# Softmax sums of four units collected in one tile, heads turned two units at a time

## The chip, the cores and the metric

The kernel runs on one core of a Trainium2 chip. The metric is the device time of one execution in microseconds (us); lower is better. PE is TensorE, DVE is VectorE, ACT is ScalarE, POOL is GpSimd, SP is SyncE, which issues DMAs.

## The reference

The kernel computes one pre-norm transformer block in fp32: eight sequences of 1024 tokens, width 512, 16 heads of 32 channels. The attention is a differential one. Queries and keys of a head are cut into two halves of 16 channels, and each half gets its own softmax:

```python
h = layernorm(x)
q, k, v = split(h @ w_qkv)
a1 = softmax(q1 @ k1.T * scale)
a2 = softmax(q2 @ k2.T * scale)
out = (a1 - lam * a2) @ v               # per head: 1024 x 32
out = out / rms(out) * norm_w * 0.2     # rms over the 32 channels
x = x + reshape(out) @ wo
x = x + ffn(layernorm(x))               # ternary weights, relu squared, a low-rank branch
```

The change concerns the step from the unnormalised products `exp(scores) @ v` and the sums of the exponentials to `a1 @ v - lam * a2 @ v`.

## The kernel before

**Units.** Attention is cut into 256 units: one head and one half (512) of the queries of one sequence. A sequence ("batch" below) has 32 units. Unit u belongs to batch u // 32; i stands for u % 32. Four units (two heads) are one group n = u // 4; a group ends in one tile `og` that is normalised (`rms_squares`, `rms_sums`, `rms_apply`) and multiplied by `wo` (`output_rows`).

**Blocks.** A unit has eight key chunks kc. The loop takes two chunks at a time, so a unit is four blocks, and a block issues on PE, in this order: scores and their shift for two chunks (`exp_scores`, L267, for both softmaxes), between them four products of the maximum search of two units ahead (`max_scores`, L207), then what the order of the work has put in this slot, then the products with v (`values`, L290) of the block before. ACT takes the exponentials from PSUM (L273). DVE reduces the maximum products (L218, four per block). POOL adds the four `e` tiles of a unit up to `es` (`add_up`, L283 and L285, three additions per unit; two in the light units).

**Slots.** All engines but SP run in the order that the program writes (`manual_schedule`). In the slot behind kc 0 and 1 of a unit there stand, in this order: a step of the next batch's preparation if it is a long one (`project`, L157, or `value_tile`, L145: eight matmul instructions), `max_turn` (L232), `heads_out` (L324), steps of the group's normalisation (`later`), `sums` (L290), and a short step of the preparation (`turn_tile`, L137). The PE part of each is issued there; the part that empties its PSUM bank ("post": copies, L165, L236, L237, L334 to L347) is issued on ACT and DVE behind the whole slot, in the same order. i = 18 to 30 have a projection in this slot; 4, 6, 8, 10, 12, 14, 16 and 17 a value tile; the odd units from 3 to 15 a turn. Units with i = 16, 20, 24, 28 have a second step behind kc 4. The last batch (units 224 to 255) prepares only the first FFN tokens. It has light units, the odd ones and the last three, whose POOL sum leaves out the fourth `e` tile; PE takes that tile itself in `sums`.

**PSUM.** `one_bank()` takes one of four banks (pool `a_ps_1`). Scores, projections, turns, sums and heads share these four; a tile may be written when the last reader of the tile that had its bank is done. The maximum products have three banks of their own, `acc` one.

**The path of the sums.** `sums(u)` multiplies `es` by a tile of ones of 32 columns. With the queries in four quarters along the partitions this gives 128 x 256 sums, each repeated in 32 rows. ACT copies them to SBUF next to the unnormalised heads (`avs`, two halves of 256). `heads_out(u)` turns both halves with four transposes (two for the heads, two for the sums); DVE takes reciprocals (two), multiplies (two) and adds (one) into `og`. `sums(v)` stands in the slot of unit v + 2, `heads_out(v)` in that of v + 3; for a light v they stand behind kc 2 of v + 1 and in v + 2. A group's normalisation begins behind kc 6 of the unit in which its fourth `heads_out` stands.

Of the kernel before, what the change touches and what calls it, by code (L numbers as in the profile page):

```python
# [8 lines left out]
F32 = mybir.dt.float32  # L9
F32R = mybir.dt.float32r  # L10
AF = mybir.ActivationFunctionType
# [6 lines left out]
P = 128  # L18
# [6 lines left out]
def block_phases(  # L25
# [14 lines left out]
    nc = tc.nc  # L40
    B, S, E = x.shape
    H, HD = norm_w.shape
# [3 lines left out]
    HS = S // 2  # L46
    SCALE = float(HD) ** -0.5
    NU = B * H * 2
    ident, neg_half = consts
# [3 lines left out]
    p_s = ctx.enter_context(tc.tile_pool(name="a_s", bufs=4))  # L53
# [10 lines left out]
    wo_sb = p_wo.tile([P, KC, E], F32, name="wo_sb")  # L64
    nw = p_wo.tile([P, NHP], F32, name="nw")
    one_nlam = p_wo.tile([P, 1], F32, name="one_nlam")
    ones = p_wo.tile([P, HD], F32, name="ones")
    wv = wpool.tile([P, KC, E], F32, tag="wv", name="wv")
    nc.gpsimd.memset(ones, 1.0)

    one2 = wpool.tile([P, P], F32R, name="one2")
    nms = [wpool.tile([P, HS], F32R, name=f"nms{i}") for i in range(3)]
# [31 lines left out]
    def one_bank():  # L104
        return ps_1.tile([P, 512], F32, tag="one", name="one")
# [142 lines left out]

    e_of, es_of, acc_of, avs_of = {}, {}, {}, {}

    def exp_scores(u, kc, between=None):

# [20 lines left out]
    def light(u):  # L275

        return u >= NU - 2 * H and (u % 2 == 1 or u >= NU - 3)
# [9 lines left out]
    def quarters(out, w, e, start, stop):  # L287

        for g in range(4):
            nc.tensor.matmul(  # L290
                out[32 * g : 32 * g + 32, :], w,
                e[:, g // 2, (g % 2) * (HS // 2) : (g % 2 + 1) * (HS // 2)],
                start=start, stop=stop,
            )
# [8 lines left out]
        )  # L303

    def evict(u):
        avs_of[u] = p_s.tile([P, 2, HS // 2], F32, tag="avs", name="avs", bufs=4)

        nc.scalar.activation(avs_of[u][:, 0, :], acc_of.pop(u), AF.Copy, scale=one_nlam)

    def sums(u):  # L310
        ps = one_bank()
        es = es_of.pop(u)
        parts = [t[:, i] for t in ((es, e_of[u, 3]) if light(u) else (es,)) for i in range(2)]
        for i, part in enumerate(parts):
            quarters(ps[:, 0 : HS // 2], ones, part, i == 0, i == len(parts) - 1)
        return lambda: nc.scalar.copy(avs_of[u][:, 1, :], ps[:, 0 : HS // 2])

    def heads_out(u):

        avs = avs_of.pop(u)  # L320
        to = one_bank()
        for i in range(2):
            for c in range(2):
                nc.tensor.transpose(  # L324
                    to[:, (2 * i + c) * P : (2 * i + c + 1) * P],
                    avs[:, i, c * P : (c + 1) * P], ident,
                )

        def post():

            parts = to.rearrange("p (i c s a d) -> p i s c a d", i=2, c=2, s=2, a=2)
            rc = p_s.tile([P, 2, 2, 2], F32, tag="rc", name="rc")
            for sm in range(2):
                nc.vector.reciprocal(rc[:, sm], parts[:, 1, sm, :, :, 0])  # L334
            o2 = p_s.tile([P, 2, 2, HD], F32, tag="o2", name="o2", bufs=2)
            for sm, o in enumerate((parts[:, 0, 0], o2)):
                nc.vector.tensor_mul(
                    o, parts[:, 0, sm],
                    rc[:, sm].rearrange("p c (a o) -> p c a o", o=1)
                    .to_broadcast([P, 2, 2, HD]),  # L340
                )
            n = u // 4
            if u % 4 == 0:
                og_of[n] = p_o.tile([P, 4, P], F32, tag="og", name="og")
            col = (u % 4) * HD
            og = og_of[n][:, :, col : col + HD]
            nc.vector.tensor_add(  # L347
                og.rearrange("p (a c) d -> p c a d", a=2), parts[:, 0, 0], o2
            )

        return post

# [234 lines left out]
    adds, outs = {}, {}  # L587
    for v in range(NU):
        adds.setdefault((v + 1, 2) if light(v) else (v + 2, 0), []).append(v)
        outs.setdefault((v + 2, 0) if light(v) else (v + 3, 0), []).append(v)  # L590
    done = None
    ctx.enter_context(tc.manual_schedule(engines=engines))
    with tc.tile_pool(name="a_e", bufs=5) as p_e, tc.tile_pool(name="a_es", bufs=2) as p_es:
        for s in range(0, NS * NU + 2, 2):
            u, kc = divmod(s, NS)
            um, im = divmod(s + AHEAD, NS)
            if done is not None:
                evict(done)
                done = None
            if u > NU - 2 * H and kc == 0:  # L600
                prep.fetch()
            if u == NU - 1 and kc == 0:

                m1 = nms[(NU - 3) % 3].rearrange("p (k r) -> p k r", k=KC)
                nc.sync.dma_start(
                    m1.bitcast(F32), prep.m1_d.rearrange("p k i r -> p k (i r)")
                )
            if um < NU:
                if im == 0 and um + 1 < NU:
                    if um % 2 == 1:  # L610
                        load_keys(um // 2 + 1)
                    load_queries(um + 1)
                between, first = max_scores(um, im, apart=True)
            else:
                between = first = None
            if u < NU:
                if u % (2 * H) == 0 and kc == 0:
                    assert not fill
                    fill = prepare(u // (2 * H) + 1) if u + 2 * H < NU else prepare_tokens()
                exp_scores(u, kc, between=between)  # L620
                if first:
                    first()
                exp_scores(u, kc + 1)
                add_up(u, kc)
            reduce = max_scores(um, im + 1) if um < NU else None
            posts = []

            if fill and (kc == 0 or kc == 4 and u % (2 * H) >= H and u % 4 == 0):
                prepare_step, long = fill.pop(0)
            else:  # L630
                prepare_step = None
            if prepare_step and long:
                posts.append(prepare_step())
            if kc == 0 and um <= NU:
                posts.append(max_turn(um - 1))
            for v in outs.pop((u, kc), []):
                posts.append(heads_out(v))
                if v % 4 == 3:
                    n = v // 4
                    later[u, 6] = lambda n=n: rms_squares(n)  # L640
                    later[u + 1, 0] = lambda n=n: rms_sums(n)
                    later[u + 1, 2] = lambda n=n: rms_apply(n)
                    later[u + 2, 4] = lambda n=n: output_rows(n)
            if (u, kc) in later:
                posts.append(later.pop((u, kc))())
            for v in adds.pop((u, kc), []):
                posts.append(sums(v))
            if prepare_step and not long:
                posts.append(prepare_step())
            if reduce:  # L650
                reduce()
            if 2 <= s < NS * NU + 2:
                uv, kv = divmod(s - 2, NS)
                values(uv, kv)
                values(uv, kv + 1)
                if kv == NS - 2:
                    done = uv
            for post in posts:
                if post:
                    post()  # L660
        evict(done)
        whole(lambda: sums(NU - 1))
    assert not later and list(adds.values()) == list(outs.values()) == [[NU - 1]]

# [104 lines left out]
    def output(g, ys, tiles=range(4)):  # L769
# [16 lines left out]

    n = NU // 4 - 1
    rest = {
        0: lambda: heads_out(NU - 1), 1: lambda: rms_squares(n), 2: lambda: rms_sums(n),
        3: lambda: rms_apply(n),  # L790
        5: lambda: output_rows(n, lambda: ps_mx.tile([P, 512], F32, tag="mx", name="py")),
    }
    low_rank(0)

# [319 lines left out]
```

## Time and profile before

| what | value |
|---|---|
| runs (three) | 5340.47, 5342.63, 5344.19 us; median 5342.63 us |
| span of the profiled execution | 5338.5 us, 4.1 us under that median (its own time outside the span is not recorded) |
| PE busy | 5280.1 us (99%), 41522 matmuls |
| POOL busy | 4121.0 us (77%) |
| DVE busy | 3787.7 us (71%) |
| ACT busy | 2832.5 us (53%) |
| attention loop, first to last exponential | 140.0 to 4261.4 us |
| one batch of 32 units in the middle | 522.3 us |

"Busy" counts the time in which at least one instruction of the engine ran. A matmul's recorded duration contains its way through the array, and matmuls overlap: what a matmul costs is read from the distance between starts. "x16" behind a row of the timeline means that 16 instructions of the same line were merged, and the second column is then the time from the first's start to the last's end.

### The profile page before, as it was taken

Reading aid. Unit: us, or ns where it says so; the run is one execution under the profiler, and the core shown is the slowest. Engines: PE = TensorE matmul, PEld = TensorE weight load, DVE = VectorE, ACT = ScalarE, POOL = GpSimd, SP = SyncE. Lnnn points to the kernel's source line nnn. Section 1 sums busy time; section 2 is a strip of 40 time slices with the busy share of each in tenths; the row PEclk is TensorE's granted clock in tenths of the full one; section 3 lists DMA queues with packets and bytes.
Section 4 is the critical chain, followed back from the end, with each engine's and each line's share of the span. In section 5 each row is a group of like instructions: output and inputs, shape, how many; then the busy total and the mean of one; then the engine's idle time right before and its main releaser. Section 6 shows DMA issues by size and latency. Waiting matters only on the chain.

```text
span 5338.5 us, 105587 instructions
## 1 busy us (share of the span) xinstructions
PE 5280.1 (99%) x41522; PEld 3243.9 (61%) x41522; DVE 3787.7 (71%) x7599; ACT 2832.5 (53%) x5502; POOL 4121.0 (77%) x1495
## 2 busy tenths in 40 slices
PE   8999999999999999999999999999999999999999
PEld 4555555555555555555555555555555578888887
DVE  6877787777778777877777777777888645555554
ACT  4665566566656665666566656655666522222221
POOL 0898899889988998899899989998888733333333
PEclk9999999999999999999999999999999999999999
DMA  8112211211121112111211121112211101111111
GB/s 275 47 55 74 71 50 55 75 66 55 54 77 65 52 57 77 64 55 56 75 65 50 60 81 57 56 61 78 100 48 44 50 31 32 32 32 32 32 32 32
DMA packets 185246, 328.48 MB, mean 62 GB/s; under 512 B 33312, under 2 KB 55840, under 8 KB 184112
## 3 DMA queue, kind: packets, MB, share of 16 engines
q1 hardware_dynamic: 183824, 319.12, 18.3%
q8 instruction: 329, 5.39, 0.4%
q0 software_dynamic: 544, 2.10, 0.1%
q14 instruction: 165, 1.35, 0.1%
q10 hardware_dynamic: 384, 0.52, 0.0%
HBM read 209.16 MB, written 112.46 MB: 60 GB/s over the span
## 4 chain that ended last, share of the span: by engine, by line
PE 84%; POOL 11%; DVE 3%; issue 1%; ACT 1%; DMA 0%; SPq 0%; POOLq 0%; DVEq 0%; ACTq 0%
PE acc L290 15%; PE one L267 14%; PE mx L207 13%; PE y L763 9%; PE pf L744 8%; PE one L157 8%; POOL es L285 6%; PE one L290 4%; PE one L145 4%; PE one L383 3%; POOL es L283 3%; PE one L324 2%; DVE nm L218 1%; PE pf L748 1%; POOL ss L369 1%
## 5 line engine op out<-in xcount | busy, mean ns | idle before, releaser
L218 DVE TENSOR_REDUCE nm<-mx 128x1 f32<-128x512 f32 x4096 | 2550.3, 683 | 256.6 <-PE mx L207 251.5
L273 ACT ACTIVATE e<-one 128x512 f32<-128x512 f32 x4096 | 2116.5, 603 | 803.2 <-PE one L267 751.1
L285 POOL TENSOR_TENSOR es<-es,e 128x2048 f32<-128x2048 f32 x495 | 2261.3, 4568 | 63.2 <-ACT e L273 31.1
L207 PE MATMUL mx<-tk,tq 64*128 64x512 f32 x4096 | 1453.1, 444 | 6.2 <-DVE nm L218 5.6
L283 POOL TENSOR_TENSOR es<-e 128x2048 f32<-128x2048 f32 x256 | 1169.6, 4569 | 278.3 <-ACT e L273 278.2
L267 PE MATMUL one<-nms,one 64*128 64x512 f32 x4096 | 1175.8, 420 | 5.1 <-ACT e L273 2.7
L290 PE MATMUL acc<-e,v 128*32 128x256 f32 x16384 | 1092.7, 384 | 0.0
L207 PEld LDWEIGHTS mx<-tk,tq 64*128 64x128 f32 x4096 | 750.9, 184 | 549.0 <-DVE nm L218 312.3
L267 PE MATMUL one<-tq,tk 64*128 64x512 f32 x4096 | 1063.6, 392 | 0.0
L753 POOL TENSOR_TENSOR r<-r 128x512 f32<-128x512 f32 x256 | 268.4, 1050 | 639.2 <-ACT r L752 618.8
L290 PEld LDWEIGHTS acc<-e,v 128*32 128x32 f32 x16384 | 450.0, 109 | 433.7 <-issue 179.0
L267 PEld LDWEIGHTS one<-tq,tk 64*128 64x128 f32 x4096 | 580.2, 185 | 82.6
L752 ACT ACTIVATE r<-pf,s_fc 128x512 f32<-128x512 f32 x256 | 176.1, 688 | 794.6 <-PE pf L748 544.2
L267 PEld LDWEIGHTS one<-nms,one 64*128 64x128 f32 x4096 | 515.2, 184 | 80.5 <-DVE og L347 15.5
L763 PE MATMUL y<-wpr,r 128*128 128x512 f32 x2048 | 523.3, 397 | 3.7 <-DVE r L757 1.7
L756 DVE CAST r<-r 128x512 fp32r<-128x512 f32 x256 | 180.4, 705 | 425.9 <-POOL r L753 425.9
L157 PE MATMUL one<-hT,wqk 128*128 128x512 f32 x1024 | 475.4, 607 | 1.5 <-ACT hT L138 1.5
L763 PEld LDWEIGHTS y<-wpr,r 128*128 128x128 f32 x2048 | 375.0, 188 | 98.6 <-DVE o L773 20.1
L744 PE MATMUL pf<-hTh,wfc 128*128 128x512 f32 x1024 | 398.8, 389 | 0.0
L744 PE MATMUL pf<-hTl,wfc 128*128 128x512 f32 x1024 | 398.6, 389 | 0.0
L165 DVE SCALAR_TENSOR_TENSOR pc<-one,pc 128x512 fp32r<-128x512 f32 x128 | 88.5, 692 | 350.9 <-ACT pc L164 350.9
L157 PEld LDWEIGHTS one<-hT,wqk 128*128 128x128 f32 x1024 | 185.0, 190 | 217.3 <-issue 187.9
(137 smaller groups left out, 4284.1 us busy)
## 6 DMA issues: line engine op xcount, KB each, us to landing
qk<-pc SPq DMA_DIRECT2D x128, 512.0 KB
tq<-qk SPq DMA_DIRECT2D x512, 128.0 KB
tk<-qk SPq DMA_DIRECT2D x256, 256.0 KB
xs<-in_L_attn_x SPq DMA_DIRECT2D x64, 256.0 KB
xr<-in_L_attn_x SPq DMA_DIRECT2D x256, 64.0 KB
x_dram<-y SPq DMA_DIRECT2D x64, 256.0 KB
out<-o SPq DMA_DIRECT2D x248, 64.0 KB
nms<-md SPq DMA_DIRECT2D x512, 4.0 KB
```

The source lines that it names most:

```text
L145: nc.tensor.matmul(pv, hT_of[b][:, kc, c * P : (c + 1) * P], wv[:, kc, :], start=(kc == 0), stop=(kc == KC - 1),)
L157: nc.tensor.matmul(ps, wqk[:, kc, c0 : c0 + P], hT_of[b][:, kc, tok], start=(kc == 0), stop=(kc == KC - 1),)
L207: nc.tensor.matmul(mx[sm], tq[rows, c * P : (c + 1) * P], tk[rows, kh * 512 : kh * 512 + 512], start=True, stop=True,)
L218: nc.vector.tensor_reduce(nm_of[u][:, kh, sm, c : c + 1], mx[sm], AX.X, ALU.max, negate=True)
L267: nc.tensor.matmul(st[sm], w[rows, cols], m[rows, :], start=(w is one2), stop=(w is not one2))
L273: nc.scalar.activation(e[:, kc % 2, sm, :], st[sm], AF.Exp)
L283: nc.gpsimd.tensor_add(es_of[u], e_of[u, 0], e)
L285: nc.gpsimd.tensor_add(es_of[u], es_of[u], e)
L290: nc.tensor.matmul(out[32 * g : 32 * g + 32, :], w, e[:, g // 2, (g % 2) * (HS // 2) : (g % 2 + 1) * (HS // 2)], start=start, stop=stop,)
L744: nc.tensor.matmul(pf, w[:, kc, :], hT, start=(kc == 0 and i == 0), stop=False)
L753: nc.gpsimd.tensor_mul(r, r, r)
L763: nc.tensor.matmul(ys[i], r2[:, i * P : (i + 1) * P], prep.wpr[j // (NJ // 2)][:, j % (NJ // 2), :], start=(j == 0 and k == 0), stop=(j == ...
```

## The change

The ones become four blocks of 32 columns. In block k only columns 8k to 8k + 7 are one. `sums(u)` uses block u % 4, so that the sums of unit u stand in rows 8k to 8k + 7 of each quarter and zeros in the others. The first unit of a group is copied to a tile `ssum` by ACT; the other three are added to it by DVE from PSUM. `sums_out(n)` turns `ssum` with two transposes and takes all reciprocals of the group in one DVE instruction of 128 x 32. `heads_out` turns two units at a time (four transposes) and multiplies them together: two multiplications of 128 x 256 in place of four of 128 x 128, and two additions into `og`, as before. `sums_out` and the first `heads_out` of group n stand in the slot of unit 4n + 6, the second `heads_out` in that of unit 4n + 7, and the normalisation begins one unit later than before, so that `output_rows` falls in units with u % 4 = 1 and not 0. In light groups all three stand in unit 4n + 5. After the last unit they are spread over the first steps of the FFN.

```diff
-    ones = p_wo.tile([P, HD], F32, name="ones")
+    ones = p_wo.tile([P, 4, HD], F32, name="ones")
-    nc.gpsimd.memset(ones, 1.0)
+    nc.gpsimd.memset(ones, 0.0)
+    for k in range(4):
+        nc.gpsimd.memset(ones[:, k, 8 * k : 8 * k + 8], 1.0)
...
     def evict(u):
-        avs_of[u] = p_s.tile([P, 2, HS // 2], F32, tag="avs", name="avs", bufs=4)
-        nc.scalar.activation(avs_of[u][:, 0, :], acc_of.pop(u), AF.Copy, scale=one_nlam)
+        avs_of[u] = p_s.tile([P, HS // 2], F32, tag="avs", name="avs", bufs=5)
+        nc.scalar.activation(avs_of[u], acc_of.pop(u), AF.Copy, scale=one_nlam)
...
-            quarters(ps[:, 0 : HS // 2], ones, part, i == 0, i == len(parts) - 1)
-        return lambda: nc.scalar.copy(avs_of[u][:, 1, :], ps[:, 0 : HS // 2])
+            quarters(ps, ones[:, u % 4], part, i == 0, i == len(parts) - 1)
+        def post():
+            n = u // 4
+            if u % 4 == 0:
+                ssum_of[n] = p_s.tile([P, HS // 2], F32, tag="ssum", name="ssum", bufs=2)
+                nc.scalar.copy(ssum_of[n], ps)
+            else:
+                nc.vector.tensor_add(ssum_of[n], ps, ssum_of[n])
+        return post
+    def sums_out(n):
+        ss = ssum_of.pop(n)
+        ts = one_bank()
+        for c in range(2):
+            nc.tensor.transpose(ts[:, c * P : (c + 1) * P], ss[:, c * P : (c + 1) * P], ident)
+        def post():
+            rc_of[n] = p_s.tile([P, 4, 2, 4], F32, tag="rc", name="rc", bufs=2)
+            nc.vector.reciprocal(
+                rc_of[n].rearrange("p k c g -> p c g k"),
+                ts[:, 0 : 2 * P].rearrange("p (c g k r) -> p c g k r", c=2, g=4, k=4)[..., 0],
+            )
+        return post
...
     def heads_out(u):
-        avs = avs_of.pop(u)
+        n, k = divmod(u, 4)
         to = one_bank()
         for i in range(2):
+            avs = avs_of.pop(u + i)
             for c in range(2):
                 nc.tensor.transpose(
                     to[:, (2 * i + c) * P : (2 * i + c + 1) * P],
-                    avs[:, i, c * P : (c + 1) * P], ident,
+                    avs[:, c * P : (c + 1) * P], ident,
                 )
...
-        outs.setdefault((v + 2, 0) if light(v) else (v + 3, 0), []).append(v)
+        if v % 4 == 3:
+            n, soon = v // 4, light(v)
+            outs.setdefault((v + 2, 0) if soon else (v + 3, 0), []).extend(
+                [lambda n=n: sums_out(n), lambda v=v: heads_out(v - 3)]
+            )
+            outs.setdefault((v + 2, 0) if soon else (v + 4, 0), []).extend(
+                [lambda v=v: heads_out(v - 1), n]
+            )
...
     rest = {
-        0: lambda: heads_out(NU - 1), 1: lambda: rms_squares(n), 2: lambda: rms_sums(n),
-        3: lambda: rms_apply(n),
-        5: lambda: output_rows(n, lambda: ps_mx.tile([P, 512], F32, tag="mx", name="py")),
+        0: lambda: sums_out(n), 1: lambda: heads_out(NU - 4), 2: lambda: heads_out(NU - 2),
+        3: lambda: rms_squares(n), 4: lambda: rms_sums(n), 5: lambda: rms_apply(n),
+        7: lambda: output_rows(n, lambda: ps_mx.tile([P, 512], F32, tag="mx", name="py")),
     }
```

More of the change, by code (lines that the diff above doesn't have):

```diff
@@ L247, in max_turn @@
         return post
-    e_of, es_of, acc_of, avs_of = {}, {}, {}, {}
+    e_of, es_of, acc_of, avs_of, ssum_of, rc_of = {}, {}, {}, {}, {}, {}
     def exp_scores(u, kc, between=None):
@@ L305, in evict @@
     def evict(u):
-        avs_of[u] = p_s.tile([P, 2, HS // 2], F32, tag="avs", name="avs", bufs=4)
-        nc.scalar.activation(avs_of[u][:, 0, :], acc_of.pop(u), AF.Copy, scale=one_nlam)
+        avs_of[u] = p_s.tile([P, HS // 2], F32, tag="avs", name="avs", bufs=5)
+        nc.scalar.activation(avs_of[u], acc_of.pop(u), AF.Copy, scale=one_nlam)
     def sums(u):
-        ps = one_bank()
+        ps = one_bank()[:, 0 : HS // 2]
         es = es_of.pop(u)
@@ L325, in heads_out @@
                     to[:, (2 * i + c) * P : (2 * i + c + 1) * P],
-                    avs[:, i, c * P : (c + 1) * P], ident,
+                    avs[:, c * P : (c + 1) * P], ident,
                 )
         def post():
[L331 to L336, printed above, removed]
+            parts = to.rearrange("p (m s a d) -> p s m a d", m=4, s=2, a=2)
+            rc = rc_of[n].rearrange("p k c (s a) -> p s (k c) a", s=2)[:, :, 2 * k : 2 * k + 4]
+            o2 = p_s.tile([P, 4, 2, HD], F32, tag="o2", name="o2", bufs=1)
+            for sm, o in enumerate((parts[:, 0], o2)):
                 nc.vector.tensor_mul(
-                    o, parts[:, 0, sm],
-                    rc[:, sm].rearrange("p c (a o) -> p c a o", o=1)
-                    .to_broadcast([P, 2, 2, HD]),
-                )
-            n = u // 4
-            if u % 4 == 0:
+                    o, parts[:, sm],
+                    rc[:, sm].rearrange("p m (a o) -> p m a o", o=1)
+                    .to_broadcast([P, 4, 2, HD]),
+                )
+            if k == 0:
                 og_of[n] = p_o.tile([P, 4, P], F32, tag="og", name="og")
[L345 to L349, printed above, removed]
+            for i in range(2):
+                og = og_of[n][:, :, (k + i) * HD : (k + i + 1) * HD]
+                nc.vector.tensor_add(
+                    og.rearrange("p (a c) d -> p c a d", a=2),
+                    parts[:, 0, 2 * i : 2 * i + 2], o2[:, 2 * i : 2 * i + 2],
+                )
         return post
@@ L589, in block_phases @@
         adds.setdefault((v + 1, 2) if light(v) else (v + 2, 0), []).append(v)
-        outs.setdefault((v + 2, 0) if light(v) else (v + 3, 0), []).append(v)
+        if v % 4 == 3:
[5 more added lines that the diff above has]
+                [lambda v=v: heads_out(v - 1), n]
+            )
     done = None
@@ L635, in block_phases @@
                 posts.append(max_turn(um - 1))
[L636 to L639, printed above, removed]
+            for turn in outs.pop((u, kc), []):
+                if callable(turn):
+                    posts.append(turn())
+                else:
+                    n = turn
                     later[u, 6] = lambda n=n: rms_squares(n)
@@ L662, in block_phases @@
         whole(lambda: sums(NU - 1))
-    assert not later and list(adds.values()) == list(outs.values()) == [[NU - 1]]
+    assert not later and list(adds.values()) == [[NU - 1]] and len(outs) == 1
     HID, R, NJ = prep.HID, prep.R, prep.NJ
```

## The prediction

> **What bounds the kernel now.** I read the page first, then busy time by stretches, then the timeline of single slots. About 0.2% of 5342.63 us, 10.7 us, is what a measurement of this kernel can tell from no change.
>
> ```profile
> PE 5280.1 (99%) x41522; PEld 3243.9 (61%) x41522; DVE 3787.7 (71%) x7599; ACT 2832.5 (53%) x5502; POOL 4121.0 (77%) x1495
> 1157.69:1447.50 289.81, 287.02 (x2621) 162.98 (x2615) 229.50 (x476) 187.19 (x365) 283.85 (x96) 1.00 0.17 52
> 1447.50:1680.22 232.72, 232.72 (x1933) 130.86 (x1935) 169.05 (x342) 132.89 (x260) 194.69 (x49) 1.00 0.22 75
> ```
>
> The second and third line are two stretches of one batch: length, then busy time of PE, PEld, DVE, ACT, POOL. In the first (i = 30 to i = 17 of the next batch) POOL works 283.85 of 289.81 us without a gap over 0.1 us; in the second (i = 18 to 30) it has 38 us to spare and PE none. Where POOL sets the pace, it does so through the `e` tiles: i = 10 of batch 2 starts its exponentials when POOL's last addition of i = 8 ends (1321.21 + 4.59 = 1325.80):
>
> ```profile
> 1321.21 4.59 POOL L285 TENSOR_TENSOR es<-es,e 128x2048 f32<-128x2048 f32 x1
> 1325.90 1.09 ACT L273 ACTIVATE e<-one 128x512 f32<-128x512 f32 x2 [0.66 <-PE one L267]
> ```
>
> Next the slot of unit 50 (i = 18, a projection ahead of it):
>
> ```profile
> 935.34 0.27 PE L232 MATMUL one<-ident,nm 128*8 128x128 f32 x1
> ...
> 935.45 0.60 PE L324 MATMUL one<-ident,avs 128*128 128x128 f32 x4
> 935.54 0.60 ACT L164 ACTIVATE pc<-one 128x512 fp32r<-128x512 f32 x1 [2.54 <-PE one L157]
> ...
> 935.98 1.07 PE L290 MATMUL one<-es,ones 128*32 128x256 f32 x16
> 936.17 0.69 DVE L165 SCALAR_TENSOR_TENSOR pc<-one,pc 128x512 fp32r<-128x512 f32 x1 [3.05 <-ACT pc L164]
> ...
> 937.08 0.28 DVE L237 TENSOR_TENSOR mt<-one,mt 8x128 fp32r<-8x128 f32 x1
> 937.29 0.23 DVE L334 RECIPROCAL rc<-one 128x4 f32<-128x4 f32 x2
> 937.55 0.30 DVE L337 TENSOR_TENSOR one<-one,rc 128x128 f32<-128x128 f32 x1
> ...
> 937.84 0.49 PE L207 MATMUL mx<-tk,tq 64*128 64x512 f32 x1
> ...
> 937.88 0.29 DVE L337 TENSOR_TENSOR o<-one,rc 128x128 f32<-128x128 f32 x1
> 938.21 0.29 DVE L347 TENSOR_TENSOR og<-one,o 128x128 f32<-128x128 f32 x1
> 938.42 0.68 DVE L218 TENSOR_REDUCE nm<-mx 128x1 f32<-128x512 f32 x1
> ```
>
> Call 935.34 T0. Four transposes take 935.98 - 935.45 = 0.53 us of PE, 0.133 each. The next block starts at T0 + 2.50, DVE's first maximum 0.58 us behind it. An undisturbed block takes 2.70 us with that distance 0.54; the maximum products have three banks, so what DVE starts later than 0.54 is added to the block. In the last batch this already costs 1.27 us (1.81 - 0.54; the block is 3.97 long), since two units are turned in one slot:
>
> ```profile
> 3984.01 1.15 PE L324 MATMUL one<-ident,avs 128*128 128x128 f32 x8
> 3986.09 0.49 PE L207 MATMUL mx<-tk,tq 64*128 64x512 f32 x1
> 3987.90 2.47 DVE L218 TENSOR_REDUCE nm<-mx 128x1 f32<-128x512 f32 x4
> 3990.06 0.50 PE L207 MATMUL mx<-tk,tq 64*128 64x512 f32 x1
> ```
>
> **The change, part by part.** Below "0" to "3" is u % 4.
>
> *Transposes.* 1024 become 640; 384 x 0.133 = 51 us of PE go. By slot: units 0 and 1 lose four (-0.53; -0.59 where no long step stands ahead), unit 2 gains the two of `sums_out` (+0.27), unit 3 is as before.
>
> The Trainium skill ("TensorE: Matmul & The Clock Gate", Part 4) gives about 275 ns for a transpose in a kernel. The rows' durations agree (278 ns), but their starts are 133 ns apart; by the page 106 us would go, and I keep 51.
>
> *Copies and DVE.* 192 ACT copies of 0.37 us go, on an engine that waits for PE. DVE gets 192 additions and loses half of its small multiplications. The nearest row to a 256-wide one is
>
> ```profile
> L549 DVE TENSOR_TENSOR hTl<-wb,hTh 128x256 fp32r<-128x256 f32 x120 | 45.0, 417 | 0.0
> ```
>
> against 300 and 292 ns for 128 (L337): +0.13 us for 128 more. So 0.43 and 0.42 for the multiplications, 0.42 for the addition; bounds 0.30 (no cost by width) and 0.60 (twice). The reciprocal of 128 x 32 is near L334's 151 ns: 0.18 (0.15 to 0.3).
>
> *Unit 2 with a projection (i = 18, 22, 26, 30): a fifth bank.* Projection, maximum, sums turned, heads turned and sums want five banks, and there are four. The changed program's first product of `sums` waits for the projection's own second reader, L165: it ends at 936.86, T0 + 1.52, and a waiting PE starts 0.05 later (the median of such waits), T0 + 1.57. Six transposes would let it start at T0 + 0.11 + 0.80 = 0.91. Behind it on PE are the sums, `values` and all later blocks. Cost 0.66, with the transposes 0.93, less 0.04 of DVE lateness that PE's delay covers: +0.89. Bounds: +0.23, if the bank came free in time, to +1.0 with a cold start of the weight loads (0.11). Value tiles have one reader, ACT, ready at T0 + 0.84: no wait.
>
> *Unit 3 with a projection (i = 19, 23, 27): a longer DVE queue.* Behind L237 (T0 + 2.02) stand two multiplications, two additions and the addition of the sums: 0.43 + 0.42 + 0.29 + 0.29 + 0.42 with 0.03 between, to T0 + 4.02. The first maximum overlaps the end by 0.08 and starts at T0 + 3.94, where T0 + 2.50 + 0.54 was due: 0.90 late. Before it was 0.10 late there (the group's `ss` reduction stood in the same slot). +0.80; bounds +0.41 and +1.29 from the widths.
>
> The Trainium skill ("Perfetto Trace Analysis", Optimizing Scalar/DVE Operations) speaks for grouping where the engine is saturated, and for breaking up instructions where it isn't but causes bubbles elsewhere. This DVE is 71% busy and is the second case.
>
> *Units 0 and 1 with a projection.* DVE is free at T0 + 2.4, the block (now T0 + 1.97) needs it at 2.51: -0.53 and -0.04 of old lateness, -0.57 each. Without a projection DVE is free sooner.
>
> *Normalisation one unit later.* `output_rows` (3.6 us of PE) leaves the unit that has two projections; its four loads and its store pass SP's key and query loads of one unit, with DMA engines 22% busy and no one waiting. POOL's `rms_apply` (0.21 + 2.92 + 1.05 = 4.2 us) moves behind the first addition of the next unit; between i = 30 and i = 6, 6 and 10, 10 and 14 POOL has as many of them as before. Zero.
>
> **Sums.** Batches 1 to 6, from POOL's first addition of i = 30 to the start of i = 10: POOL's chain is unchanged, 0. From i = 10 to 14 the units take 62.29 us, POOL's additions for them 62.02; PE alone would fall to 61.4, so POOL decides: -0.27. i = 14 to 17: +0.27, 0, -0.53, -0.53. i = 18 to 29: 3 x (0.89 + 0.80 - 0.57 - 0.57) = +1.65. i = 30: +0.89. Sum +1.48, six times +8.9.
>
> Batch 0 starts without POOL's backlog: three groups of 0.27 - 0.53 - 0.59 = -0.85 instead of -0.27: 1.48 + 0.27 - 2.55 = -0.8.
>
> Last batch: unit 3 loses eight transposes and its wait, -1.08 - 1.34 = -2.42. In unit 1 DVE has the reciprocal and both pairs one behind the other: from T0 + 1.81 0.18 + 2 x 1.43 with 0.03 between, less two overlaps of 0.08, first maximum at T0 + 4.94 instead of 4.15, +0.79. Six groups -9.8. POOL's light sum of unit 231 ends at 3913.49 and PE uses it at 3915.78; with PE 2.42 sooner POOL holds it by 0.2: six times, +1.2. The first units -1.0: 227 turns one pair less (-0.53 and 1.1 of DVE), 228 no longer waits for POOL (-0.43), 229 has +1.04. Unit 255 -2.4, 256 -0.5. In the FFN stand ten transposes for four (+0.8) and an estimated 0.5 for their banks. Sum -11.2.
> Total 8.9 - 0.8 - 11.2 = -3.1. The profiled 5338.5 becomes 5335.4, with the 4.1 around it 5339.5; I say 5339, on its own 5330 to 5350.
>
> **Rivals.**
> (1) *One of the new waits doesn't come*, because the order of readers is kinder than I read it. Without the fifth bank's wait 28 x 0.66 = 18 us less (5321); without DVE's lateness 21 x 0.90 = 19 less (5320); without either 5302. For it: PE is 99% busy, and by that row alone 51 us should go. Against: the program's own wait, and L165's end at T0 + 1.52.
> (2) *The wide DVE instructions cost twice the narrow ones*; slower. The queue of unit 3 grows by 0.17 + 0.16 + 0.16 = 0.49, 21 times; in the last batch 0.66, seven times; i = 15 becomes 0.34 late, seven times: +17, 5357. It decides from 0.57 us per instruction on. Against: the 417 ns above.
> (3) *The last batch gives nothing back*, since POOL's light sums hold PE as soon as it is faster: +11, 5350. Against: they had 2.3 us to spare, so most of the 2.42 should come.
> That the sums are not collected is excluded: the changed program has 640 of these transposes.
>
> **How the numbers follow.** Forecast 0.55, (1) 0.25, (2) 0.13, (3) 0.07. Faster: (1) and the low edge of the forecast, 0.30. Slower: (2) and the upper edges, 0.19. Same: 0.51. The range reaches to one wait missing and to (2): 5318 to 5356; both waits missing lies outside.
>
> **What would show it.** Batches of 523 to 525 us in the middle (522.3 before); the four units from i = 18 longer by about 0.5 than 70.7; in unit 2 with a projection, the sums' first product 0.05 behind the end of the projection's second reader; in i = 19 a first block of 3.6 us; i = 6 to 10 still 62.2; groups of 56.6 us in the last batch (58.1 before). I am wrong if i = 18 to 30 gets shorter (a wait missing), if the first stretch of POOL opens gaps, or if 128 x 256 takes over 0.5 us.

## The result

The changed kernel takes 5350.83 us (median of 19 runs, 5348.65 to 5353.27), the kernel before 5340.69 us beside it (19 runs, 5338.77 to 5346.14). The ratio is 1.0018, with a 95% interval of 1.0011 to 1.0025: slower, by ten microseconds, with 384 transposes taken away (51 us of PE by the prediction's estimate). The profiled execution spans 5349.1 us, 10.6 more than before's 5338.5.

These are the first lines of the page and the chain of waits by engine, after the change:

```profile
PE 5245.8 (98%) x41138; PEld 3211.3 (60%) x41138; DVE 3779.9 (71%) x7087; ACT 2761.0 (52%) x5310; POOL 4123.0 (77%) x1499
PE 75%; POOL 18%; DVE 3%; issue 2%; ACT 1%; DMA 0%; SPq 0%; POOLq 0%; DVEq 0%; ACTq 0%
```

384 instructions are gone from PE and its busy time fell by 34 us, but the span grew: PE now waits. The chain runs over PE for 75% of the span (84% before) and over POOL for 18% (11% before). That is half of the story. The other half is in the lengths of the parts, from the first exponential of one batch to that of the next:

| part (us) | before | after | difference | forecast |
|---|---|---|---|---|
| up to the first exponential | 140.03 | 140.20 | +0.2 | 0 |
| batch 0 | 509.76 | 511.05 | +1.3 | -0.8 |
| batches 1 to 6, mean | 522.24 | 524.48 | +2.24, six times 13.4 | +1.48, six times 8.9 |
| batch 7, to its last exponential | 478.15 | 469.68 | -8.5 | together |
| the rest (feed-forward) | 1077.07 | 1081.25 | +4.2 | -11.2 |

To see what sets a batch's length, cut it where POOL begins the first addition of a unit. Two windows, first of before, then of after: unit 0 to unit 16 of batch 4, and unit 18 to unit 30. The columns are the length, then busy time of PE, PEld, DVE, ACT, POOL, each with its instructions, the granted clock, the DMA share and GB/s.

```profile
2230.96:2478.26 247.30, 244.80 (x2240) 139.17 (x2237) 196.10 (x405) 161.64 (x315) 242.22 (x83) 1.00 0.17 52
2507.69:2719.90 212.21, 212.21 (x1742) 118.75 (x1742) 152.64 (x310) 119.77 (x234) 176.47 (x45) 1.00 0.22 76
```

```profile
2235.14:2482.46 247.32, 241.44 (x2216) 137.79 (x2214) 195.43 (x374) 156.59 (x303) 242.24 (x82) 1.00 0.17 52
2516.28:2730.57 214.29, 212.04 (x1724) 115.95 (x1724) 152.57 (x286) 116.47 (x225) 176.60 (x45) 1.00 0.22 76
```

In the first window the length is the same to 0.02 us, with POOL busy for all but the 5 us between its instructions: PE's work falls by 3.4 us and all of it becomes PE's waiting. In the second, PE's work is hardly less, 2.2 us of waiting are new, and the stretch is 2.1 us longer. So nothing was gained where PE got less to do, and time was lost where PE decides.

**Unit 2 with a projection.** The timeline of the same slot that the prediction showed, unit 50:

```profile
936.30 0.27 PE L234 MATMUL one<-ident,nm 128*8 128x128 f32 x1
...
936.63 0.60 PE L352 MATMUL one<-ident,avs 128*128 128x128 f32 x4
937.13 0.69 DVE L167 SCALAR_TENSOR_TENSOR pc<-one,pc 128x512 fp32r<-128x512 f32 x1 [3.06 <-ACT pc L166]
...
937.97 1.07 PE L292 MATMUL one<-es,ones 128*32 128x256 f32 x16 [0.74 <-DVE pc L167]
...
939.69 0.49 DVE L371 TENSOR_TENSOR og<-one,o 128x128 f32<-128x128 f32 x2
939.83 0.49 PE L209 MATMUL mx<-tk,tq 64*128 64x512 f32 x1
940.36 0.69 DVE L220 TENSOR_REDUCE nm<-mx 128x1 f32<-128x512 f32 x1 [0.19 <-PE mx L209]
```

The fifth bank is there: the first product of `sums` waits 0.74 us for the projection's second reader L167 and starts 0.15 behind its end. The block is 8.78 us long (7.75 before), +1.03.

**Unit 3 with a projection.** DVE's queue in the slot of unit 51, whose next block begins at 955.71 on PE:

```profile
955.15 0.41 DVE L362 TENSOR_TENSOR one<-one,rc 128x256 f32<-128x256 f32 x1
955.60 0.42 DVE L362 TENSOR_TENSOR o<-one,rc 128x256 f32<-128x256 f32 x1
956.06 0.49 DVE L371 TENSOR_TENSOR og<-one,o 128x128 f32<-128x128 f32 x2
956.47 0.41 DVE L325 TENSOR_TENSOR ssum<-one,ssum 128x256 f32<-128x256 f32 x1
956.80 1.88 DVE L220 TENSOR_REDUCE nm<-mx 128x1 f32<-128x512 f32 x3
```

The maximum starts 1.09 behind the block where 0.54 is undisturbed, and the block is 3.25 us long (2.81 before): +0.44. By groups, the mean duration in ns being the number behind the bar and the busy time:

```profile
L325 DVE TENSOR_TENSOR ssum<-one,ssum 128x256 f32<-128x256 f32 x192 | 79.0, 411 | 57.2 <-PE one L292 57.2
L362 DVE TENSOR_TENSOR o<-one,rc 128x256 f32<-128x256 f32 x128 | 54.4, 425 | 4.4
L338 DVE RECIPROCAL rc<-one 128x32 f32<-128x32 f32 x64 | 21.6, 337 | 0.0
```

**The end.** Unit 255's wait for POOL, and the granted clock behind it (last but two column of the windows, ahead of the DMA share):

```profile
4254.38 1.54 PE L292 MATMUL one<-es,ones 128*32 128x256 f32 x16 [3.90 <-POOL es L287]
4255.68 1.95 PE L292 MATMUL one<-e,ones 128*32 128x256 f32 x16
```

```profile
4245.00:4250.00 5.00, 5.00 (x53) 2.58 (x51) 0.00 (x0) 4.52 (x11) 4.75 (x5) 1.00 0.00 0
4254.38:4258.80 4.42, 4.42 (x50) 2.16 (x50) 0.43 (x1) 0.00 (x0) 4.42 (x1) 0.61 0.00 0
```

Sixteen products take up to 1.95 us here; in other places they take 1.07. The kernel before has the same wait, shorter, and behind it slow products and a clock of 0.67 too:

```profile
4248.33 1.94 PE L290 MATMUL one<-es,ones 128*32 128x256 f32 x16 [1.84 <-POOL es L285]
4248.33:4252.50 4.17, 4.17 (x50) 1.97 (x51) 0.00 (x0) 0.37 (x1) 4.17 (x1) 0.67 0.00 0
```

In the feed-forward part PE's first products for `y` waited 1.94 us before, for their own operands. Now they wait for posts of `heads_out` that stand on DVE behind casts, and the granted clock falls behind these waits (last line):

```profile
4282.42 0.69 DVE L790 TENSOR_TENSOR r<-r,r 128x512 fp32r<-128x512 f32 x1
4283.03 0.43 DVE L362 TENSOR_TENSOR one<-one,rc 128x256 f32<-128x256 f32 x1
...
4284.58 0.71 PE L796 MATMUL y<-wpr,r 128*128 128x512 f32 x2 [2.35 <-DVE og L371]
...
4286.97 1.19 PE L796 MATMUL y<-wpr,r 128*128 128x512 f32 x2 [1.68 <-DVE og L371]
4286.97:4292.39 5.42, 5.42 (x13) 4.26 (x14) 0.00 (x0) 0.35 (x1) 0.00 (x0) 0.50 0.01 3
```

### The profile page after: what moved, and what is told of

It is laid out like the page before. It is cut to its first block, busy times and chain, and to the rows that moved or that the text cites. A ratio compares the mean times of both kernels' runs of the same rounds, so it can differ in the third digit from the quotient of the medians.

```text
span 5349.1 us, 104112 instructions
## 1 busy us (share of the span) xinstructions
PE 5245.8 (98%) x41138; PEld 3211.3 (60%) x41138; DVE 3779.9 (71%) x7087; ACT 2761.0 (52%) x5310; POOL 4123.0 (77%) x1499
## 4 chain that ended last, share of the span: by engine, by line
PE 75%; POOL 18%; DVE 3%; issue 2%; ACT 1%; DMA 0%; SPq 0%; POOLq 0%; DVEq 0%; ACTq 0%
PE acc L292 13%; PE one L269 12%; PE mx L209 11%; POOL es L287 10%; PE y L796 8%; PE one L159 8%; PE pf L777 8%; POOL es L285 4%; PE one L292 4%; PE one L147 3%; PE one L408 3%; POOL ss L394 1%; DVE nm L220 1%; PE pf L781 1%; ACT e L275 1%
## 5 line engine op out<-in xcount | busy, mean ns | idle before, releaser
L167 DVE SCALAR_TENSOR_TENSOR pc<-one,pc 128x512 fp32r<-128x512 f32 x128 | 88.5, 692 | 348.3 <-ACT pc L166 348.3
```

## The experiments

The theory: the change pays with three new waits (the fifth bank, DVE's queue in unit 3, the turns in the feed-forward part), and its saving stays hidden behind POOL in the first half of each batch and in the last units. The general rival: PE or DVE simply has more to do in these slots, and the waits are only where that shows. Lengths of single units below are from the traces, as a mean over batches 1 to 6.

**1. No fifth bank.**

```diff
     def max_turn(u):
-        tr = one_bank()
+        tr = turn_bank[0] = one_bank()
...
-        ts = one_bank()
+        ts = turn_bank[0][:, 2 * P : 4 * P] if n < NU // 4 - 8 else one_bank()
```

> The changed kernel, but in units 2 the turned sums go into columns 256 to 511 of the bank in which the maxima are turned, so that four banks are wanted in that slot and not five; nothing else is moved. My theory (the fifth bank's wait costs 0.75 us in each of the 28 slots with a projection): in the trace the sums' first product of unit 50 starts about 0.9 us after the turning of the maxima instead of 1.67, the block of that slot is about 8.0 us long instead of 8.78, each middle batch about 3.0 us shorter than the changed kernel's 524.46, and the whole about 20 us shorter, 5331 (5327 to 5336), ratio to the kernel before 0.998. Rival (the longer slot is the two extra transposes and a later DVE queue, whichever bank they use): the block stays above 8.5 and the whole within 4 us of 5350.

Measured: 5339.96 us, ratio to before 0.9999 (0.9990 to 1.0008). A middle batch is 1.57 us shorter than after's, half of what I expected. The slot of unit 50:

```profile
933.59 0.27 PE L235 MATMUL one<-ident,nm 128*8 128x128 f32 x1
...
934.45 1.07 PE L293 MATMUL one<-es,ones 128*32 128x256 f32 x16
...
936.31 0.50 PE L210 MATMUL mx<-tk,tq 64*128 64x512 f32 x1
...
936.97 0.49 DVE L372 TENSOR_TENSOR og<-one,o 128x128 f32<-128x128 f32 x2
937.38 0.68 DVE L221 TENSOR_REDUCE nm<-mx 128x1 f32<-128x512 f32 x1
```

The wait is gone: the sums start at 0.86 instead of 1.67 behind the turning, the next block 0.81 sooner. But DVE's queue (reciprocal, two multiplications, two additions) ends where it did, and the first maximum now starts 1.07 behind the block, 0.53 late. Each such unit gains 0.23 to 0.29 us, not 0.75. The bank's wait was covering a second one. That two causes stood one behind the other was not in the theory.

**2. The addition out of unit 3.**

```diff
+            elif u % 4 == 1 and not light(u):
+                kept[n] = p_s.tile([P, HS // 2], F32, tag="kept", name="kept", bufs=1)
+                nc.scalar.copy(kept[n], ps)
             else:
+                if n in kept:
+                    nc.vector.tensor_add(ssum_of[n], ssum_of[n], kept.pop(n))
                 nc.vector.tensor_add(ssum_of[n], ps, ssum_of[n])
```

(`ssum` also has one buffer instead of two, to make room.)

> The changed kernel, but the addition of the second unit's sums is taken out of DVE's queue in the slot of unit 3: ACT copies them to a tile of their own and DVE adds them one unit later, in the slot of unit 0, where it is idle. My theory (in unit 3 with a projection the next maximum waits for the end of DVE's queue, 0.42 us too late in each of 21 slots): the first block of unit 51 comes down from 3.25 to about 2.85 us, each middle batch is 1.3 us shorter, the whole 8 to 9 us, 5342 (5339 to 5346). Rival (the lateness there comes from the two multiplications' place in the queue and the readers of the banks, and the addition hides beside PE): within 3 us of 5350.

Measured: 5385.9 us, ratio 1.0084 (1.0071 to 1.0098); a middle batch is 4.8 us longer than after's. Unit 3 did get shorter, by 0.28 to 0.34, but unit 0 grew by 1.3 to 1.45. DVE and then POOL in the slot of unit 52:

```profile
976.78 1.62 DVE L330 TENSOR_TENSOR ssum<-ssum,kept 128x256 f32<-128x256 f32 x1
978.51 0.42 DVE L331 TENSOR_TENSOR ssum<-one,ssum 128x256 f32<-128x256 f32 x1
```

```profile
968.92 9.19 POOL L288 TENSOR_TENSOR es<-es,e 128x2048 f32<-128x2048 f32 x2
980.69 4.55 POOL L286 TENSOR_TENSOR es<-e 128x2048 f32<-128x2048 f32 x1 [2.58 <-ACT e L276]
```

The two additions have the same shape. The one with an operand in PSUM takes 0.42 us; the one with both in SBUF ends at 978.40, 0.29 behind the end of POOL's addition at 978.11. Over its 56 executions it takes 0.46 to 2.65 us, and wherever POOL is in an addition when it starts, it ends 0.28 to 0.29 us after the end of that addition. The Trainium skill ("SBUF — State Buffer", SBUF: two separate sides) describes this: DVE and GpSimd share one pair of ports as an exclusive lock, and of a DVE operation with two SBUF inputs and a GpSimd operation that reads SBUF the one that starts first holds the pair for its whole length, while the other is blocked. This run agrees with it. As a test of the theory it is inconclusive, since it put in a larger wait than it removed; experiment 12 takes the question up again.

**3. The last turns ahead of the feed-forward part.**

```diff
-        0: lambda: sums_out(n), 1: lambda: heads_out(NU - 4), 2: lambda: heads_out(NU - 2),
-        3: lambda: rms_squares(n), 4: lambda: rms_sums(n), 5: lambda: rms_apply(n),
-        7: lambda: output_rows(...),
+        1: lambda: rms_squares(n), 2: lambda: rms_sums(n), 3: lambda: rms_apply(n),
+        5: lambda: output_rows(...),
     }
     low_rank(0)
+    for step in (lambda: sums_out(n), lambda: heads_out(NU - 4), lambda: heads_out(NU - 2)):
+        whole(step)
```

> The changed kernel, but the last group's sums and heads are all turned ahead of the first step of the feed-forward part, and the normalisation follows two steps sooner. My theory (the feed-forward part is 4.2 us longer than before because its first y products wait for two banks whose readers stand in DVE's queue behind casts that wait for POOL): the two waits of 2.35 and 1.68 us go, the stretch behind the last exponential falls from 1081.2 to about 1077.5 us, the whole by 3 to 4 us, 5347. Rival (the y products wait for POOL's squares anyway, and the banks only look like the cause): the stretch stays above 1080.

Measured: 5345.41 us, ratio 1.0007 (0.9997 to 1.0016). The stretch behind the last exponential falls from 1081.25 to 1074.01, 7.2 us and more than expected (3 us less than before, too); the loop in front is unchanged to 0.15 us a batch. The `y` products now wait for their own operands:

```profile
4282.30 0.51 PE L796 MATMUL y<-wpr,r 128*128 128x512 f32 x1 [0.90 <-DVE r L789]
...
4283.84 1.89 PE L796 MATMUL y<-wpr,r 128*128 128x512 f32 x7 [1.04 <-DVE r L790]
4283.84:4290.00 6.16, 6.16 (x27) 5.11 (x28) 2.95 (x6) 0.69 (x1) 1.34 (x2) 1.00 0.00 0
```

4.03 us of waiting became 1.94, a wait for `us` of 0.75 is gone too, and the granted clock stays at 1.00. In the changed kernel it was 0.50 for 5.42 us of PE's work, which costs half of that, 2.7 us, by estimate. So the cause is shown: the order of the last turns, through the waits that it makes and the clock behind them. Some 1.7 us of the gain are left that I did not follow.

**4. The second preparation step beside the output rows again.** Both stand behind kc 4; the expectations of 4 and 5 call this the fifth block, it is the third of the unit's four.

```diff
-            if fill and (kc == 0 or kc == 4 and u % (2 * H) >= H and u % 4 == 0):
+            if fill and (kc == 0 or kc == 4 and u % (2 * H) >= H and u % 4 == 1):
```

> The changed kernel, but the second preparation step of a group, in the second half of each batch, comes in unit 1 (fifth block) instead of unit 0, so that it shares its slot with the group's output rows as in the kernel before. My theory (the later normalisation separated two long steps that used to share one slot, which costs 0.2 us per group of the second half, because the end of a long step is a block of its own that starts late): the two slots together take 12.5 us instead of 12.7, each middle batch is 0.6 to 0.8 us shorter than 524.46, the whole about 5 us, 5346. Rival (long steps cost the same together and apart, and the 0.2 us came from elsewhere in these units): middle batches stay at 524.4, the whole at 5350.

Measured: 5346.94 us, ratio 1.0012 (1.0003 to 1.0020). Units 20 and 21, 24 and 25, 28 and 29 together are 0.19, 0.18 and 0.21 us shorter; 16 and 17 are 0.18 longer. A middle batch is 0.38 us shorter, in the direction of the theory and half its size, because the first of the four groups went the other way.

**5. The turns in a long block.** `sums_out` and the first `heads_out` in unit 1, behind kc 4, beside the output rows of the group before; the second in unit 2; none in unit 3. Experiment 4's edit is part of it.

```diff
-            outs.setdefault((v + 2, 0) if soon else (v + 3, 0), []).extend(
+            outs.setdefault((v + 2, 0) if soon else (v + 2, 4), []).extend(
                 [lambda n=n: sums_out(n), lambda v=v: heads_out(v - 3)]
...
-            outs.setdefault((v + 2, 0) if soon else (v + 4, 0), []).extend(
+            outs.setdefault((v + 2, 0) if soon else (v + 3, 0), []).extend(
...
-                    later[u + 2, 4] = lambda n=n: output_rows(n)
+                    later[u + 3 - light(4 * n + 3), 4] = lambda n=n: output_rows(n)
```

> The changed kernel with other places for the turns: the sums and the first two units of a group are turned in unit 1, fifth block, beside the output rows of the group before (and, in the second half of a batch, beside the second preparation step, which moves there from unit 0); the other two units are turned in unit 2, first block, and none in unit 3. My theory (the cost is the DVE queue and the banks of the first blocks of units 2 and 3, and a block with output rows has room on DVE for both): with a projection, unit 2's block falls from 8.78 to about 8.0, unit 3 loses 0.9, and the fifth block of unit 1 grows by the 0.8 of its six transposes; each middle batch about 3 us shorter than the changed kernel's 524.46, the whole 20 to 25 us shorter, 5328 (5322 to 5335). Rival (the DVE work of the turns costs its own length wherever it stands): the fifth block of unit 1 grows by 2 us or more, and the whole stays within 5 us of 5350.

Measured: 5345.23 us, ratio 1.0006 (0.9998 to 1.0015). Where projections run it does what was expected: unit 2 -0.82, unit 3 -0.98, units 0 and 1 together +0.45, and from unit 18 to 30, cut as above, 210.3 us for after's 214.3. But a whole batch is on average only 1.1 us shorter. POOL's stretch from unit 0 to 16 grew from 247.3 to 248.3 in batches 1 and 4 (247.4 to 247.5 in the other four), and the two stretches at its ends (30 to 0 and 16 to 18) together from 62.8 to 65.4 in all six, with 2.5 us more idle time on POOL between 16 and 18. The normalisation falls into other units there; I have not taken that apart further.

**6 and 7. Less for POOL, in unit 30 alone.** The same edit in before (6) and after (7): `light` gets a wider companion for the additions and the sums.

```diff
+    def short(u):
+        return light(u) or u % (2 * H) == 2 * H - 2
...
-        elif kc == 4 or kc == 6 and not light(u):
+        elif kc == 4 or kc == 6 and not short(u):
...
-        adds.setdefault((v + 1, 2) if light(v) else (v + 2, 0), []).append(v)
+        adds.setdefault((v + 1, 2) if short(v) else (v + 2, 0), []).append(v)
```

> The kernel before, but in unit 30 of every batch POOL leaves out its last addition, and PE multiplies that tile by ones itself (8 products more, 0.54 us, in the next unit's third block); POOL has 4.6 us less to do in the stretch from i = 30 to i = 13. My theory (POOL and PE need nearly the same time in that stretch of the kernel before): PE's added work and POOL's relief nearly cancel, each middle batch between 1 us shorter and 1 us longer than 522.2. Rival (POOL is not the pace there): each batch 0.5 to 1 us longer, the same as in the changed kernel with this edit.

> The changed kernel with the same edit: in unit 30 of every batch POOL leaves out its last addition and PE does it with 8 products more. My theory (in the stretch from i = 30 to i = 13 PE has become faster by 0.85 us per group, and POOL withholds it): the stretch gets shorter by some 2 to 3 us per batch, batch 0 included, the whole by about 17 us, 5334 (5328 to 5342). Rival (the transposes that left the units without a projection were never worth anything there, for a reason other than POOL): each batch 0.5 to 1 us longer, the whole 5355.

Measured: before becomes 5333.45 us, ratio 0.9984 (0.9975 to 0.9992); after becomes 5340.64, ratio 0.9998 (0.9989 to 1.0008), 10 us below the changed kernel. A middle batch gets 0.75 us shorter in before and 1.31 in after, not 0 and 2 to 3. The trace tells why it doesn't tell the cases apart: of the 4.6 us taken from POOL, 3.2 to 3.3 reappear as POOL's idle time in unit 31, because POOL had caught up there. From unit 4 on in after, and from unit 7 on in before, every unit is as long as without the edit, with POOL busy again. Some 4 us of after's gain lie in the last batch, whose unit 226 falls from 20.96 to 16.84 us.

**9 and 10. Less for POOL in units 2, 6, 10, 14 and 30.**

```diff
-        return light(u) or u % (2 * H) == 2 * H - 2
+        return light(u) or u % (2 * H) in ((2, 6, 10, 14, 30) if u < NU - 2 * H else (30,))
```

> The kernel before, with POOL's last addition left to PE (8 products by ones, 0.54 us) not in unit 30 alone but in units 2, 6, 10, 14 and 30 of each batch, so that POOL has 4.6 us per group of four to spare in the first half of a batch too. My theory (from unit 0 to unit 16 POOL alone sets the length, 247.3 us in both kernels; without it PE would need 62.3 us per group here and 61.4 in the changed kernel): POOL gets gaps of several us per group in that stretch; each batch stays within 1 us of the 521.4 that the edit in unit 30 alone gave, since PE gets the added products and has no saving to show. Rival (POOL's additions are only the visible part of a pace that something else sets): each batch 2 us longer, 0.54 us for each of the four.

> The changed kernel with the same edit in units 2, 6, 10, 14 and 30. My theory: without POOL's pace the 0.85 us per group that the transposes save in units without a projection come to light, 3 to 4 us per batch; each batch falls from the 523.1 of the edit in unit 30 alone to about 520, below the kernel before with the same edit, the whole to about 5318 (5310 to 5328). Rival (PE has saved nothing there, because DVE's queue took it): each batch 523 to 525, still 1.5 to 2.5 us longer than the kernel before with the same edit, the whole 5340 to 5350.

Measured: 5376.06 us (ratio 1.0069, 1.0055 to 1.0083) and 5373.49 us (1.0058, 1.0046 to 1.0071). Both became slower, against my forecast of the level: in before a sum moved to PE costs 0.85 us in its group and not 0.54, and in unit 3 PE waits for POOL itself (in batch 3 1.75 us in before, 2.90 in after), since the edit also asks for POOL's result three blocks sooner. Nor is the changed kernel's batch the shorter one, as the theory had it: 527.92 us against 527.03. What the pair was for can be read in units 4 to 15 alone, for instance in units 8 to 11 of batch 3. First before, then after, without the edit:

```profile
1815.63:1877.89 62.26, 62.26 (x568) 35.38 (x566) 49.42 (x103) 40.66 (x79) 60.92 (x22) 1.00 0.17 53
```

```profile
1821.82:1883.88 62.06, 61.46 (x562) 35.10 (x560) 49.18 (x95) 39.57 (x76) 60.72 (x22) 1.00 0.17 53
```

And with it, before and after:

```profile
1835.93:1899.09 63.16, 63.16 (x584) 35.94 (x582) 49.42 (x103) 40.67 (x80) 56.26 (x21) 1.00 0.17 53
```

```profile
1836.39:1898.75 62.36, 62.26 (x578) 35.61 (x576) 49.20 (x95) 39.56 (x77) 56.31 (x21) 1.00 0.17 53
```

With POOL at 56.3 of 62 to 63 us PE is busy without a gap (but for 0.1 us in the changed kernel), and the changed kernel is 0.80 us faster in this group. With POOL at its full load the difference is 0.20. As a mean of batches 1 to 6, from first exponential to first exponential, the three groups from unit 4 to 15 are 0.81, 0.89 and 0.61 us shorter in the changed kernel with the edit, and -0.06, 0.29 and -0.03 without it. That is the saving, and POOL withholds it: shown for these three groups. In the whole batch it doesn't show, because with the edit units 0 to 3 are 1.0 us longer in the changed kernel (the longer wait in unit 3) and units 16 to 31 still 2.2.

**8. The last normalisation but one behind POOL's additions.**

```diff
-                    later[u + 1, 2] = lambda n=n: rms_apply(n)
+                    later[u + 1, 6 if u == NU - 3 else 2] = lambda n=n: rms_apply(n)
```

> The changed kernel, but the normalisation of the last group but one on POOL (its three instructions, 4.2 us) comes in the last block of unit 254 instead of the third, behind POOL's additions for that unit. My theory (the saving of the last two units was taken by a wait of 3.90 us for POOL, which has this normalisation between its additions): the wait falls to under 1 us, the last batch from 469.68 to about 466.5, the whole to 5348. Rival (the sums of unit 254 wait for POOL's additions themselves, whose tiles come late): the wait stays above 3 us, or the output rows wait for the normalisation instead, and the last batch stays at 469.7.

Measured: 5343.71 us, ratio 1.0004 (0.9996 to 1.0013). Batch 7 falls from 469.68 to 464.30, 5.4 us, where the wait alone could give 3.7. The same products as shown above:

```profile
4251.22 1.07 PE L292 MATMUL one<-es,ones 128*32 128x256 f32 x16 [0.21 <-ACT e L275]
4252.08 1.07 PE L292 MATMUL one<-e,ones 128*32 128x256 f32 x16
4251.22:4254.00 2.78, 2.78 (x50) 1.78 (x50) 0.42 (x1) 1.33 (x3) 2.71 (x1) 1.00 0.00 0
```

Without the long wait the clock stays at 1.00 and sixteen products take 1.07 us; after's 0.61 over 4.42 us had cost another 1.7 us (by estimate 4.42 x 0.39, which with the wait makes the 5.4).

**12. The sums' additions on DVE twice.**

```diff
-                ssum_of[n] = p_s.tile([P, HS // 2], F32, tag="ssum", name="ssum", bufs=2)
+                ssum_of[n] = p_s.tile([P, HS // 2], F32, tag="ssum", name="ssum", bufs=1)
                 nc.scalar.copy(ssum_of[n], ps)
             else:
+                twin = p_s.tile([P, HS // 2], F32, tag="twin", name="twin", bufs=1)
+                nc.vector.tensor_add(twin, ps, ssum_of[n])
                 nc.vector.tensor_add(ssum_of[n], ps, ssum_of[n])
```

> The changed kernel with every addition of the sums on DVE done twice (once into a tile that nobody reads), 0.41 us each from PSUM, 0.33 with the overlap. My theory (in unit 3 with a projection DVE's queue is what PE waits for, in units 0 and 1 the addition hides): the first block of unit 51 grows from 3.25 to about 3.6, units 0 and 1 with a projection by 0.1 or less; where POOL sets the pace nothing; the four units from i = 18 are 0.5 to 0.6 longer, each middle batch 1.7 longer than 524.46, and the whole, with the last batch, 10 to 17 us longer, 5362. Rival (DVE's queue is not what PE waits for in unit 3, and its block is long for the turns and their banks alone): middle batches stay within 0.5 us.

Measured: 5368.15 us, ratio 1.0054 (1.0037 to 1.0071). Unit 3 with a projection is 0.45 longer, three times the same, units 0 and 1 by 0.11 and 0.10, unit 2 by 0; a middle batch by 2.06. DVE in unit 51:

```profile
959.23 0.41 DVE L326 TENSOR_TENSOR twin<-one,ssum 128x256 f32<-128x256 f32 x1
959.67 0.42 DVE L327 TENSOR_TENSOR ssum<-one,ssum 128x256 f32<-128x256 f32 x1
960.01 1.87 DVE L220 TENSOR_REDUCE nm<-mx 128x1 f32<-128x512 f32 x3
```

So in unit 3 an addition on DVE is paid in full, in units 0 and 1 three quarters of it hide. This is what experiment 2 was to show. (The one buffer for `ssum` makes room for `twin`; unit 2, whose slot has the copy of the first unit's sums and no addition, kept its length.)

**11. The repairs together**: 1, 3, 4, 8 and the edit in unit 30, no line besides.

> The changed kernel with the repairs that helped one by one: the turned sums in the bank of the maxima, the second preparation step beside the output rows, the last group's turns ahead of the feed-forward part, the last normalisation but one behind POOL's additions, and the edit in unit 30. If their savings add up (per batch 1.57 + 0.38 + 1.31, in the feed-forward part 7.2, in the last batch 5.4 and 4.2), each middle batch comes to 521.2, the rest after the last exponential to 1074, the whole to 5311 (5306 to 5318), 0.995 of the kernel before. If the normalisation's and the edit's savings in the last batch are one and the same wait for POOL, 4 us more.

Measured: 5317.52 us, ratio to before 0.9954 (0.9941 to 0.9966): faster than both kernels, by 23 and by 33 us. A middle batch is 521.6 us (521.2 expected) and batch 7 459.6, the sum of the two savings there. Of the 6 us more than expected some 3 are batch 0, which at 511.15 gained nothing (it pays for the edit in unit 31 and has no shorter start), 2 the middle batches and 2 the rest behind the last exponential, 1076.4 instead of 1074; batch 7 and the start give some 2 back. The general rival falls with experiments 1 and 3: they leave the work as it is and move it, and the time falls.

## Why the prediction was wrong

I said 5339 us, no measurable change; it was 5350.8. The sum was -3.1 in the trace's terms and the trace has +10.6. The direction in the middle batches was right, and both new waits came. What failed are three terms: the last units and the hand-over to the feed-forward part, where the sum took PE alone to decide; the middle batches, where it put the later normalisation at zero and the bank too low; and the saving in batch 0.

*The end (6.9 of the 13.7 us).* "Sum -11.2" for the last batch and the feed-forward part; measured -4.3. Its largest item holds: the six groups were to give 8.6 after POOL's share and gave 8.8 (units 228 to 251, most groups 58.1 to 56.6 us). The others don't: unit 255 missed by 2.7 us, the feed-forward part by 3.4. "Unit 255 -2.4, 256 -0.5" took a unit that waits for POOL as if PE alone decided there: the saving became 2.06 us more wait, 3.90 for 1.84, with some 0.3 more lost to the lower clock behind it (by estimate 4.42 x 0.39 us, against 4.17 x 0.33 before); experiment 8 takes the wait away, and 5.4 us with it. "In the FFN stand ten transposes for four (+0.8) and an estimated 0.5 for their banks" priced a bank by its transposes and not by the place of its readers in DVE's queue, and had no term for the clock behind the waits: +4.2, and experiment 3 shows that this order costs all of it.

*The middle batches (4.5).* 6 x 1.48 was forecast, 6 x 2.24 came. The fifth bank cost 1.03 per slot, at the upper bound of +1.0 that I had given and not at 0.89: the product starts 0.15 behind its releaser, not 0.05. Units 0 and 1 gave 0.44, not 0.53, since the sums start 0.20 behind the turned maxima where a transpose starts 0.11 behind. "Normalisation one unit later. ... Zero" cost 0.2 per group, because two long steps that shared a slot no longer do (experiment 4). Unit 3 was too dear in my sum: the first multiplication, the second `og` addition and the addition of the sums each start about 0.08 us before the end of the instruction ahead (the two `og` additions take 0.49 us together), where I had put 0.03 between them; the lateness is 0.55 and not 0.90, +0.44 and not +0.80. So the bank, too cheap, and unit 3, too dear, partly cancel in the sum, by luck. Experiment 12 confirms the mechanism of unit 3 and its price. The Trainium skill ("Perfetto Trace Analysis", Optimizing Scalar/DVE Operations) would break such instructions up where an engine that isn't saturated causes bubbles elsewhere; no run here broke up the grouped ones.

*Batch 0 (2.1).* "Batch 0 starts without POOL's backlog" is false. POOL's additions stand one behind the other from the batch's first units, and from units 0 to 4 it takes 59.25 us in both kernels. Its first three groups gave 0.30, 0.27 and 0.22 us, where I had 0.85 for each: the saving was withheld as in the others.

*The rivals.* (1), a wait that does not come, priced the bank at 18 us. Experiment 1 took exactly that wait away and the whole fell by 11: behind PE's wait stood DVE's, which I had worked out for unit 3 and not for unit 2, where "0.04 of DVE lateness" was covered. (2), DVE instructions at twice the narrow ones, is refuted by 411 to 425 ns; the reciprocal, though, takes 337 and not 180. (3) has nearly the measured time, 5350, and the wrong place: the light sums of the six groups did not hold PE (PE has no wait for POOL in units 228 to 254); the last unit's did.

## What to carry to other kernels

Take the queue of every engine in the slot and set its end against what the next block needs: in the kernel before, PE's transposes and DVE's posts filled the slot together, so that less work on PE alone was worth little, and a wait removed uncovered the next (0.81 us sooner on PE, 0.25 gained). A saving counts only in the stretches where its engine decides, and the last units and the hand-over between phases are stretches of their own, where the order of the last turns, with the normalisation behind them, decided 7 us here. Grouping small operations also lumps them: in unit 3 the grouped load stood ahead of an instruction that PE needed, while the units beside it had room.

## What the runs showed of the hardware that I had not expected

An elementwise addition of 128 x 256 on DVE took 0.42 us with one operand in PSUM and up to 2.65 with both in SBUF, ending 0.28 to 0.29 us behind POOL's running addition (experiment 2).

A wait of 3.90 us on PE was followed by a mean granted clock of 0.61 for 4.4 us, and cost 1.7 us besides its length; before, a wait of 1.84 us (with 0.52 of idle time shortly ahead of it) was followed by 0.67 for 4.2 us; and in the feed-forward part of the changed kernel waits of 2.35 and 1.68 us were followed by 0.50 for 5.4 us. The Trainium skill ("TensorE: Matmul & The Clock Gate", Part 1) puts the idle time that lowers the clock at about 3.4 us; both kernels show a lowered clock behind less.
